# Wider gaps between the rows of three DRAM scratch buffers in an FFT convolution kernel

## The chip, the core and the metric

The kernel runs on one core of a Trainium2 chip. The metric is the time on the device in microseconds (us), as the median of several executions. One further execution was recorded by the hardware profiler; all durations of single instructions and transfers come from that one.

The engines are named as the profile names them: PE is TensorE (matrix multiply; its weight loads are PEld), DVE is VectorE, ACT is ScalarE, POOL is GpSimd, and SP is SyncE, which here only starts DMA transfers. Transfers started by SP and ACT run in hardware queues (q1 and q10 in the profile), those started by POOL in a software queue (q0). All of them are carried out by the core's 16 DMA engines.

## What is computed

The input x is (4, 512, 512, 16) in float32: four images of 512 by 512 points with 16 channels. There are two layers, each x + layer(group norm(x)). The first is a convolution with a 512 by 512 filter per pair of channels that is given as a quotient of two polynomials, done by Fourier transform; the second is a 3 by 3 cosine-similarity convolution. Cut to what matters:

```
a = pad(denominator, ones), b = pad(numerators, zeros)          # 9 x 9 taps each
h = irfft2(rfft2(b, (512, 512)) / rfft2(a, (512, 512)))         # impulse response, 512 x 512
H = h0 + rfft2(h, (1024, 1024))                                 # per (in channel, out channel)
X = rfft2(gn(x), (1024, 1024));  Y = einsum("...hwi,ijhw->...hwj", X, H)
x = x + irfft2(Y, (1024, 1024))[:512, :512]                     # layer 0
x = x + cosine_conv3x3(gn(x))                                   # layer 1: arccos, tanh gates, bias
```

## The kernel before, in words

`body` (L1390) runs four phases one after the other. They hand data on through DRAM buffers, and the change concerns the layout of three of these.

**The buffers.** `g_d` (the filter), `x_d` (the transformed image) and `y_d` (the product) are each four DRAM tensors with 128 rows (L1391 to L1393). A row of `g_d` holds 1 MiB: 128 *places* of 8192 bytes (16 output channels j times 128 numbers). A row of `x_d` or `y_d` holds 256 KiB. The tensors are declared `PITCH` = 1024 elements wider than their content (L56), so that one row starts 4096 bytes further on than the content of the row before would end. The helper `dram(t, row, offset, *dims)` (L197) builds the access patterns: with a row given it addresses inside that row; with `None` it puts the 128 rows first, a row pitch apart, one for each SBUF partition.

**filter_phase** (L231) computes the filter pair by pair. Per output channel j, `placed` (L404) copies results into a staging tile `st` and, after eight pairs, stores it with four transfers (two halves a, two q) at L416: 128 partitions, 16 places for each, 512 bytes at each place. `odd(j)` (L422) then loads such pieces back as `ev_in` (`load`, L432, transfers at L436: 128 partitions, 4 places, 512 bytes), multiplies them with `todd` (L450), copies the result to `ot` (L455) and stores it with the same pattern into the other two tensors (L456). So all of `g_d` is written in pieces of 512 bytes, and half of it is also read in such pieces. The order of PE, DVE, ACT and POOL is fixed by hand with the class `InOrder`; SP issues its transfers in the order that the program's scheduler gives.

**forward_phase** (L604) transforms the images, and stores at L687 to `x_d` with 128 rows, 16 places 2048 bytes apart, 512 bytes each.

**conv_phase** (L697) goes over 513 filter rows (row 0 is done in two planes). In step n, SP starts four kinds of loads. `load_x(n + 3)` (L749) reads one whole row of `x_d`, 256 KiB. `load_g(n + 2)` (L737, the planes at L740) reads one whole row of `g_d`, 1 MiB, one place of 8192 bytes to each partition. `load_xe(n + 1)` (L816) reads 3 MiB from the small DRAM buffers `xf_d`, as two transfers of 1.5 MiB. Their content was computed one step earlier: `x_part` and `x_late` (L785) multiply the image row, and POOL stores it in two parts (L792, `xf_d<-xe` and `xf_d<-xl`). `xf_d` has rows of 4096 bytes at a pitch of 4608 bytes (`XP`, L58); it is not part of the change. PE does in four quarters of a step: `mix` (L846, the channel product, which reads `xe` and `gh`), `g_part` (L830, the filter's transform along the row, which reads the tile `g`), `over_q` (L867); once per step also `x_part` (L778) and `over_g` (L904), whose result POOL stores as one whole row of `y_d` (L915). The tiles `g` and `x` have two buffers, `xe` has three.

**last_phase** (L964) transforms back: for each of 16 n, eight tiles `yt` of 1 MiB are loaded at L1134 from `y_d` (128 rows, 8192 bytes from each), multiplied (L1143), and stored by ACT's queue (L1155). From n = 9 on the group norm of the second layer is prepared beside it (`prepare`, L1041), and then the 3 by 3 convolution runs.

The two address computations that the change rewrites in the filter phase are these:

```python
out=dram(g_d[h], None, a * G_ROW // 2 + ((32 * q + 16 * kp) * C + j) * 8 * C,
         [C * 8 * C, 16], [1, 8 * C]),
...
return [((first[c] + 4 * (tb % 8)) * C + j) * 8 * C for c in range(2)]
step = [C * 8 * C, 4], [1, 8 * C]
```

Of the kernel before, what the change touches and what calls it, by code (L numbers as in the profile page):

```python
# [46 lines left out]
P = 128  # L47
N = 512
B = 4
C = 16  # L50
S = 64
F = 128
G_ROW = 2 * S * C * 8 * C
X_ROW = 2 * S * B * 8 * C
Y_ROW = 2 * B * S * C * 8
PITCH = 1024  # L56
XF = F * 2 * B
XP = XF + 128  # L58
GN_EPS = 1e-5
# [137 lines left out]
def dram(t, row, offset, *dims):  # L197

    pitch = t.shape[1]
    lead = [[pitch, t.shape[0]]] if row is None else []  # L200
    return bass.AP(tensor=t.tensor, offset=t.offset + (row or 0) * pitch + offset,
                   ap=lead + [list(d) for d in dims])
# [28 lines left out]
def filter_phase(tc, cst, h0, num, den, g_d, beside):  # L231
    nc = tc.nc
    with ExitStack() as ctx:
# [170 lines left out]
        def placed(pair, st, pg):  # L404

            kp, i, h, j = (pair[0][k] for k in ("kp", "i", "h", "j"))
            for u in range(2):
                for a in range(2):
                    nc.scalar.copy(  # L409
                        st[a].rearrange("p (q k u x) i -> p u k q x i", q=2, k=2, u=2)[:, u, :, :, :, i : i + 2],  # L410
                        pg[u][:, :, :, 2 * a : 2 * a + 2].rearrange("p n k q x -> p k q x n"),
                    )
            if i == C - 2:
                for a in range(2):
                    for q in range(2):
                        nc.sync.dma_start(  # L416
                            out=dram(g_d[h], None, a * G_ROW // 2 + ((32 * q + 16 * kp) * C + j) * 8 * C,
                                     [C * 8 * C, 16], [1, 8 * C]),
                            in_=st[a].rearrange("p (q r e) i -> p q r (e i)", q=2, e=8)[:, q],
                        )  # L420

        def odd(j):  # L422

            def place(tb):
                first = ((0, 96), (64, 32))[tb // 8]
                return [((first[c] + 4 * (tb % 8)) * C + j) * 8 * C for c in range(2)]

            step = [C * 8 * C, 4], [1, 8 * C]  # L430

            def load(tb):  # L432
                ev = evp.tile([P, 2, 2, 32 * C], F32, name="ev_in")
                for h in range(2):
                    for c in range(2):
                        nc.sync.dma_start(  # L436
                            out=ev[:, h, c].rearrange("p (s e) -> p s e", s=4),
                            in_=dram(g_d[h], None, place(tb)[c], *step),
                        )
                return ev  # L440

            ev = load(0)
            for tb in range(16):
                after = load(tb + 1) if tb < 15 else None
                for hh in range(2):
                    ot = odp.tile([P, 2, 32 * C], F32, name=f"ot{hh}")
                    for c in range(2):
                        pt = ps_t.tile([P, 32 * C], F32, name="pt", tag="t")
                        for kc in range(2):
                            nc.tensor.matmul(  # L450
                                pt, todd[:, c, kc, hh * P : hh * P + P], ev[:, kc, c],
                                start=(kc == 0), stop=(kc == 1),
                            )
                        yield
                        nc.scalar.copy(ot[:, c], pt)  # L455
                        nc.sync.dma_start(  # L456
                            out=dram(g_d[2 + hh], None, place(tb)[c], *step),
                            in_=ot[:, c].rearrange("p (s e) -> p s e", s=4),
                        )
                ev = after  # L460

        def odds():

            for j in range(C):
                while done[0] < 64 * (j + 1) + 8:
                    yield
                yield from odd(j)
# [11 lines left out]
        for p in range(n_pairs + 2):  # L479
# [3 lines left out]
            if last:  # L483
                if last[0]["i"] == 0:
                    st = [stp.tile([P, N // 2, C], F32, name=f"st{a}", tag="st") for a in range(2)]
                with order:
                    for w in last:
                        edge(w)
                    placed(last, st, taps(last))
                done[0] += 2  # L490
                for w in last:
                    w.clear()
# [9 lines left out]
            with order:  # L502
# [6 lines left out]
                j, kp, r = p // 32, p // 16 % 2, p % 16  # L509
# [187 lines left out]
def conv_phase(tc, cst, g_d, x_d, y_d):  # L697
    nc = tc.nc
    with ExitStack() as ctx:
# [32 lines left out]
        def load_g(n):  # L732
            rc, r, plane = rows[n]
            g = io.tile([P, C, 8 * C], F32, name="g")
            t, w = g.rearrange("p j x -> p (j x)"), C * 8 * C
            if plane is None:
                nc.sync.dma_start(out=t, in_=dram(g_d[rc], r, 0, [w, P], [1, w]))  # L737
            else:
                for to, at in ((0, (0, 96)[plane]), (64, (64, 32)[plane])):
                    nc.sync.dma_start(out=t[to : to + 32], in_=dram(g_d[rc], r, at * w, [w, 32], [1, w]))  # L740
                    nc.gpsimd.memset(t[to + 32 : to + 64], 0.0)
            state["g", n] = g

# [179 lines left out]
        def step(n):  # L923
# [7 lines left out]
            if row(2):  # L931
                load_g(n + 2)
# [457 lines left out]
def body(tc, ins, cst, out):  # L1390
    g_d = [tc.dram_tile([P, G_ROW + PITCH], F32, name=f"g_d{r}") for r in range(4)]  # L1391
    x_d = [tc.dram_tile([P, X_ROW + PITCH], F32, name=f"x_d{r}") for r in range(4)]
    y_d = [tc.dram_tile([P, Y_ROW + PITCH], F32, name=f"y_d{r}") for r in range(4)]  # L1393
    yw_d = [tc.dram_tile([C, N, N], F32, name=f"yw_d{b}") for b in range(B)]
    t_d = [[tc.dram_tile([N, P, C], F32, name=f"t_d{b}_{w}") for w in range(4)] for b in range(B)]
    with tc.tile_pool(name="s_mv", bufs=2 * B) as mp:
        mvs = []
        with tc.tile_pool(name="s_in", bufs=1) as xp:
            beside = image_stats(tc, xp, mp, ins["x"], mvs)
            filter_phase(tc, cst, ins["L0_conv_h0"], ins["L0_conv_numerators"][0],  # L1400
                         ins["L0_conv_denumerator"], g_d, beside)
            for _ in beside:
                pass
        forward_phase(tc, cst, ins["x"], mvs, x_d)
    conv_phase(tc, cst, g_d, x_d, y_d)
    last_phase(tc, cst, ins["x"], y_d, yw_d, t_d, ins["L1_conv_kernel"], ins["L1_conv_bias"],
               ins["L1_conv_radius"], out)
# [30 lines left out]
```

## Time and profile before

| | us |
|---|---|
| median of 3 runs | 16582.36 |
| lowest and highest of them | 16561.65, 16588.23 |
| the profiled execution, its own time | 16601.06 |
| its span, first to last instruction | 16599.1 |
| filter phase, about 0 to 3950 | 3950 |
| forward phase, about 3950 to 4750 | 800 |
| conv phase, about 4750 to 13750 | 9000 |
| back transform, about 13750 to 14900 | 1150 |
| 3 by 3 convolution, about 14900 to the end | 1700 |

The profiled execution took 1.96 us more than its span, and 18.7 us more than the median. The granted TensorE clock was 0.973 of full speed over the span. The program has 2703070 packets in the hardware queue that SP feeds; a packet is one contiguous piece that one DMA engine moves.

How to read it: "busy" of an engine is the time in which it executes instructions, as a share of the span or of the window asked for. The DMA share is the mean busy share of the 16 DMA engines. A group line gives what is written and read (`out<-in`), count, busy time, mean duration in ns, idle time of the engine before it, and what ended most of that idle time. A wait line says who waited for whom, the total in us, how many times, and the longest.

### The profile page before, as it was taken

To read this page: it belongs to the slowest core of one execution; us is meant where nothing else is said; L and a number is where in the kernel's file an instruction comes from. 1 tells how busy PE (TensorE), PEld (TensorE's weight loads), DVE (VectorE), ACT (ScalarE), POOL (GpSimd) and SP (SyncE) were. 2 spreads that over 40 slices of the span, in tenths; PEclk is the share of its full clock that TensorE was granted. 3 is DMA by queue.
4 is the path that set the end of the run, shared out by engine and by line. 5 is a ranking of instruction groups with operands and counts; after the bars stand their busy time and mean duration, and the time that the engine had idled before them with its cause. 6 is when DMAs were issued, how large, how long until landed. Compare 5 with 4: busy or idle time off the path is not lost. (4 is left out here: it accounts for less than half of the span.)

```text
span 16599.1 us, 545650 instructions
## 1 busy us (share of the span) xinstructions
PE 15057.2 (91%) x232588; PEld 11240.5 (68%) x232588; DVE 10596.9 (64%) x22299; ACT 9042.9 (54%) x18799; POOL 10362.7 (62%) x10669
## 2 busy tenths in 40 slices
PE   7999999998988899889899989898888888988888
PEld 5555555554557777777777777777777777767777
DVE  8999999993545555555555555555555552357877
ACT  5666666663345555555555555555555551027888
POOL 7777777772346666666666666666666660237766
PEclk7999999999999999999999999999999999989999
DMA  4888888878878888888888888888888886885531
GB/s 134 233 235 236 232 238 235 240 226 257 253 262 327 321 328 326 326 326 323 326 328 320 328 325 329 325 323 327 319 325 328 321 324 236 309 289 167 165 108 69
DMA packets 2914698, 4543.40 MB, mean 274 GB/s; under 512 B 126114, under 2 KB 2094460, under 8 KB 2801422
## 3 DMA queue, kind: packets, MB, share of 16 engines
q1 hardware_dynamic: 2703070, 3836.37, 67.4%
q0 software_dynamic: 172336, 605.00, 9.4%
q10 hardware_dynamic: 36864, 67.13, 1.2%
q8 instruction: 1833, 30.03, 0.7%
q14 instruction: 595, 4.87, 0.1%
HBM read 3030.71 MB, written 1477.31 MB: 272 GB/s over the span
## 5 line engine op out<-in xcount | busy, mean ns | idle before, releaser
L830 PE MATMUL pg<-c_dg,g 64*128 64x128 f32 x32832 | 2851.6, 290 | 372.2 <-ACT gh L730 220.5
L846 PE MATMUL pm<-xe,gh 128*32 128x64 f32 x131328 | 2370.2, 222 | 486.0 <-issue 234.5
L830 PEld LDWEIGHTS pg<-c_dg,g 64*128 64x128 f32 x32832 | 2293.3, 189 | 716.2 <-ACT gh L730 278.1
L846 PEld LDWEIGHTS pm<-xe,gh 128*32 128x32 f32 x131328 | 1998.2, 110 | 1072.6 <-issue 838.6
L875 DVE TENSOR_TENSOR z<-zq,pz 128x256 f32<-128x256 f32 x2052 | 859.4, 419 | 2695.4 <-ACT zq L874 2641.7
L728 DVE COPY gh<-pg 128x512 f32<-128x512 f32 x2046 | 1408.3, 688 | 1148.2 <-PE pg L830 1144.1
L450 PE MATMUL pt<-ev_in,c_todd 128*128 128x512 f32 x4096 | 1927.3, 609 | 109.0 <-ACT u L338 83.4
L799 POOL TENSOR_TENSOR xu<-xe,c_late 128x256 f32<-128x256 f32 x2052 | 1392.2, 702 | 845.6 <-ACT xe L730 826.7
L507 DVE RECIPROCAL dn<-dn 128x256 f32<-128x256 f32 x1024 | 1716.9, 1716 | 0.0
L730 ACT COPY yf<-pm 128x512 f32<-128x512 f32 x2046 | 1211.9, 592 | 901.5 <-PE pm L846 887.9
L382 POOL TENSOR_TENSOR sp<-m,dn 128x512 f32<-128x512 f32 x1024 | 1301.1, 1272 | 615.0 <-DVE dn L507 528.8
L810 ACT COPY xe<-xl 64x1024 f32<-64x1024 f32 x513 | 539.1, 1051 | 1892.1 <-POOL xl L801 1892.1
L450 PEld LDWEIGHTS pt<-ev_in,c_todd 128*128 128x128 f32 x4096 | 728.6, 190 | 1021.8 <-issue 704.3
L730 ACT COPY gh<-pg 128x512 f32<-128x512 f32 x2058 | 1201.2, 584 | 356.7 <-PE pg L830 355.1
L867 PE MATMUL pz<-c_ident,yf 128*128 128x128 f32 x8208 | 1365.6, 289 | 27.1 <-issue 14.1
L398 PEld LDWEIGHTS pg<-c_dinv,sp 64*128 64x128 f32 x16384 | 1004.5, 196 | 464.6 <-ACT sp L387 210.8
L409 ACT COPY st<-pg 128x256 f32<-128x256 f32 x2048 | 617.2, 391 | 1281.2 <-PE pg L398 1281.2
L801 POOL TENSOR_TENSOR xl<-xl,xu 128x1024 f32<-128x1024 f32 x513 | 1210.0, 2359 | 40.2
L398 PE MATMUL pg<-c_dinv,sp 64*128 64x128 f32 x16384 | 1106.7, 287 | 70.4 <-ACT sp L387 47.4
L1281 PE MATMUL pc<-l_band,xn 128*128 128x160 f32 (+2 forms) x6144 | 1078.0, 334 | 50.7 <-DVE e_o L1336 50.4
L883 POOL TENSOR_TENSOR zd<-z 128x512 f32<-128x512 f32 x513 | 653.6, 1274 | 742.4 <-DVE z L875 742.3
L915 POOL DMA_DIRECT2D y_d<-yo x511 | 296.5, 580 | 1305.0 <-ACT yo L730 1279.1
(211 smaller groups left out, 30874.7 us busy)
## 6 DMA issues: line engine op xcount, KB each, us to landing
xe<-xf_d SPq DMA_DIRECT2D x1026, 1536.0 KB
g<-g_d SPq DMA_DIRECT2D x511, 1024.0 KB
g_d<-st SPq DMA_DIRECT2D x256, 1024.0 KB
ev_in<-g_d SPq DMA_DIRECT2D x1024, 256.0 KB
g_d<-ot SPq DMA_DIRECT2D x1024, 256.0 KB
xf_d<-xe POOLq DMA_DIRECT2D x513, 448.0 KB, 8.2
xf_d<-xl POOLq DMA_DIRECT2D x513, 448.0 KB, 5.5
x_d<-xo SPq DMA_DIRECT2D x128, 1024.0 KB
```

Source lines behind the costliest of these rows:

```text
L382: nc.gpsimd.tensor_mul(w["sp"], w["m"], bc(w["dn"], 2, [P, 2, 2, P]))
L398: nc.tensor.matmul(pg[u][:, n, k].rearrange("p a x -> p (a x)"), w["sp"][q, k, c, :], dinv[q, 2 * kp + k, c, :], start=(c == 0), stop=(c = ...
L450: nc.tensor.matmul(pt, todd[:, c, kc, hh * P : hh * P + P], ev[:, kc, c], start=(kc == 0), stop=(kc == 1),)
L507: nc.vector.reciprocal(w["dn"], w["dn"])
L728: nc.vector.tensor_copy(dst, src)
L730: nc.scalar.copy(dst, src)
L799: nc.gpsimd.tensor_mul(u[:, :, h, c], xe[:, :, h, 1 - c], bc(late[:, 1 + c], 2, [P, F, 2]))
L801: nc.gpsimd.tensor_add(xl.rearrange("p f h c k -> p (f h c k)"), xl.rearrange("p f h c k -> p (f h c k)"), u.rearrange("p f h c k -> p (f ...
L830: nc.tensor.matmul(pg[c][:, j % 4], g[half, j], dg[half], start=True, stop=True)
L846: nc.tensor.matmul(pm[32 * q : 32 * q + 32, g % 8], gh[:, f].rearrange("p c j -> p (c j)"), xe[:, :, f].rearrange("p t h c k -> p t (h c k ...
L867: nc.tensor.transpose(pz[:, t % 4].rearrange("p v q x -> p (v q x)"), y[:, at].rearrange("p g x -> p (g x)"), ident)
L1281: nc.tensor.matmul(pc[:, lo:hi, :].rearrange("p w j -> p (w j)"), xns[q][:, h * P + dh : h * P + dh + P], bands[dh][:, o : o + hi - lo, :] ...
```

## The change

The places of a `g_d` row lie 8704 bytes apart instead of 8192: a new constant `GP` is 128 elements (512 bytes) larger than a place's content, and every address into `g_d` uses it. A row's content with its gaps thus takes 1114112 bytes instead of 1048576. `PITCH` grows from 1024 to 1152 elements, that is from 4096 to 4608 bytes, for `g_d`, `x_d` and `y_d`. From row to row `g_d` goes from 1052672 to 1118720 bytes, and `x_d` and `y_d` go from 266240 to 266752 bytes. All of it is address arithmetic: no instruction, tile or computed number is added or removed.

```diff
-G_ROW = 2 * S * C * 8 * C
+GP = C * 8 * C + 128
+G_ROW = P * GP
...
-PITCH = 1024
+PITCH = 1152
...
-                            out=dram(g_d[h], None, a * G_ROW // 2 + ((32 * q + 16 * kp) * C + j) * 8 * C,
-                                     [C * 8 * C, 16], [1, 8 * C]),
+                            out=dram(g_d[h], None, a * G_ROW // 2 + (32 * q + 16 * kp) * GP + j * 8 * C,
+                                     [GP, 16], [1, 8 * C]),
...
-                return [((first[c] + 4 * (tb % 8)) * C + j) * 8 * C for c in range(2)]
-
-            step = [C * 8 * C, 4], [1, 8 * C]
+                return [(first[c] + 4 * (tb % 8)) * GP + j * 8 * C for c in range(2)]
+
+            step = [GP, 4], [1, 8 * C]
...
-                nc.sync.dma_start(out=t, in_=dram(g_d[rc], r, 0, [w, P], [1, w]))
+                nc.sync.dma_start(out=t, in_=dram(g_d[rc], r, 0, [GP, P], [1, w]))
...
-                    nc.sync.dma_start(out=t[to : to + 32], in_=dram(g_d[rc], r, at * w, [w, 32], [1, w]))
+                    nc.sync.dma_start(out=t[to : to + 32], in_=dram(g_d[rc], r, at * GP, [GP, 32], [1, w]))
```

## The prediction, made before the changed kernel was run

> **What bounds the kernel now.** I read the page first, then busy time by stage (us, busy time and instructions of PE, PEld, DVE, ACT and POOL, PE clock, DMA share, GB/s).
>
> ```profile
> span 16599.1 us, 545650 instructions
> PE 15057.2 (91%) x232588; PEld 11240.5 (68%) x232588; DVE 10596.9 (64%) x22299; ACT 9042.9 (54%) x18799; POOL 10362.7 (62%) x10669
> ```
>
> ```profile
> 300.00:3900.00 3600.00, 3485.57 (x28864) 2017.13 (x28863) 3203.24 (x4292) 2298.28 (x6399) 2638.78 (x3032) 1.00 0.82 236
> 3950.00:4750.00 800.00, 779.92 (x2496) 398.99 (x2496) 429.50 (x560) 273.39 (x499) 311.06 (x66) 1.00 0.78 238
> 4750.00:13750.00 9000.00, 8069.67 (x184617) 6466.92 (x184621) 4911.84 (x13312) 4771.16 (x8714) 5779.08 (x5641) 0.98 0.87 324
> 13950.00:14900.00 950.00, 840.47 (x3880) 727.41 (x3880) 391.78 (x1086) 129.99 (x298) 216.36 (x133) 0.95 0.83 290
> ```
>
> PE is busy 97% of the filter and forward stages, 90% of the conv stage (third row). DMA is busy 82, 78, 87 and 83%: high enough that each stage must be asked whether transfers end a wait. In the filter stage they hardly do; these are its longest waits for DMA:
>
> ```profile
> PEld pt L450 <- DMA ev_in<-g_d: 52.2, 163, 1.5
> ACT ot L455 <- DMA g_d<-ot: 30.7, 17, 8.6
> PEld pt L450 <- DMA g_d<-ot: 18.2, 61, 0.3
> ```
>
> In the conv stage the chain lies in one step, seen in the timeline (start us, us):
>
> ```profile
> 8000.87 0.37 SPq L816 DMA_DIRECT2D xe<-xf_d  x1
> 8001.03 1.10 PE L846 MATMUL pm<-xe,gh 128*32 128x64 f32 x64 [2.75 <-DMA xe<-xf_d]
> 8001.33 0.46 SPq L737 DMA_DIRECT2D g<-g_d  x1
> 8001.85 0.42 SPq L816 DMA_DIRECT2D xe<-xf_d  x1
> ...
> 8014.88 0.58 POOL L792 DMA_DIRECT2D xf_d<-xl  x1 [0.29 <-POOL xl L801]
> ...
> 8018.42 0.37 SPq L816 DMA_DIRECT2D xe<-xf_d  x1
> ```
>
> PE waited 2.75 us for `xe`; SP then starts half of the next `xe`, the 1 MiB of `g`, and the other half. So `g` lies in the queue ahead of data that the next row needs. The stage's SP and PE waits and its queues (packets, MB, share of 16 engines):
>
> ```profile
> SPq L816 <- DMA xf_d<-xl: 6606.7, 512, 15.1
> ```
>
> ```profile
> PE pm L846 <- DMA xe<-xf_d: 83.9, 74, 3.0
> ```
>
> ```profile
> q1 hardware_dynamic: 561699, 2287.33, 68.3%
> q0 software_dynamic: 172096, 604.21, 17.4%
> ```
>
> From the trace's packet records, sorted by queue and size: an `xe` load takes 14.9 us (median) from issue to its last packet, out of a row of 9000 / 513 = 17.5 us, and between 1 and 14 us after issue the 16 engines are full. In 189 of 513 rows the first matmul of L846 starts less than 1 us after the last `xe` packet; PE's idle time just before these sums to 157 us. In the other rows the transfer has slack (median of all: 1.5 us) and engines set the row. So the conv stage is bound partly by DMA, and a shorter `g` transfer can count there.
>
> **What the Trainium skill says.** "DMA: Bandwidth & Descriptors", section "Latency and other measured facts": copies with a 4 MiB row pitch ran at 103 GB/s, with 4 KiB more at 214, with 192 bytes more at 97. Every buffer here already has 4 KiB beyond a power of two per row, and the trace agrees that the large effect is gone: 1531509 packets of 512 bytes (300 to 3900 us) have a mean of 28.4 ns and a median of 27. Same page, "How a descriptor splits into AXI transactions": a piece is cut into 256-byte transactions, and only a start off a 256-byte boundary costs more. 8704, 4608 and the new row pitches are multiples of 256. The trace agrees for 4608: `xe`, whose DRAM rows have this pitch, has a median of 159 ns for 4096 bytes (25.8 GB/s an engine). Same page, "Issuing engines are not separate DMA queues": SP's and POOL's transfers share the 16 engines; the two shares above add to 86% of the same engines.
>
> **The change part by part.** Program order and waits on all five engines are the same in both kernels. What moves is DRAM addresses.
>
> *Filter stores and loads (L416, L456, L436).* Same 512-byte pieces. Mean 28.4 against median 27 ns: what better addresses could win is 1.4 x 1531509 / 16 = 134 us of all engines, but under a PE that is 97% busy; the cover is the idle 18% of the DMA engines. I take 0; at best the 101 us of waits shown, of which little is PE's own. If pieces got slower, the cover goes at 28.4 / 0.82 = 34.6 ns.
>
> *Forward stores (L687).* Pitch 266752 instead of 266240, same pieces; PE 780 of 800 us busy. 0, covered by the 22% that DMA is idle.
>
> *Load of a `g` row (L737).* Packets stay 8192 bytes: other loads with gaps between rows (`yt`, 260 KiB apart) come in 8192-byte packets too. 65536 such packets have a mean of 346 ns and a median of 309: the excess is 37 x 128 / 16 = 296 ns a row. It grows within a load from 314 (first 16 packets) to 379 (seventh 16), also while no other queue moves data, whereas `xe` packets settle at 160 to 165. That hints at addresses, which 512-byte gaps would spread. Against it: in the filter stage the DMA engines also work at equal residues (4 partitions apart are 4 MiB + 16 KiB) and are at their floor. So from both sides: nothing, or all 0.3 us, with another 0.13 us since the second half of `xe` starts at 187 ns a packet behind the tail of `g` and settles at 163; and below nothing, see rivals. I take half of the excess, 0.15 us a row. In the rows bound by DMA the gain is the smaller of 0.15 us and PE's idle time there, summed over the 189 rows: 27 us. Next late after that are ACT's and DVE's evictions (L730, L874), which rows with slack already wait for. As rows with slack are no shorter (17.5 us) than bound ones (17.4), part comes back; I keep 25.
>
> *`x_d` rows and `y_d` rows, whole.* Their packets are contiguous before and after; only starts move by 512 bytes a row. `x` packets have 85 against 84 ns: 0.
>
> *Loads of `yt` (L1134).* 8192-byte packets at 328 against 309 ns from 13950 to 14900: 16384 x 19 / 16 000 = 19 us of full engines, beside ACT, DVE and PE waits. I take 5; from 0 to 12.
>
> *Bases.* `g_d` grows by 33.8 MB, so `xf_d` and later buffers move. No row prices this; I take 0, inside the range.
>
> Sum: 25 + 5 = 30 us less. The profiled execution took 16601.1 (span 16599.1 plus 2.0), so it would take 16571; the median of the runs is 18.7 lower: 16582 - 30 = 16552.
>
> **The rivals.** About 0.2% (33 us) is what a measurement of this kernel can tell from no change.
>
> *All of the excess goes.* 0.43 us a row, over the bound rows 73 us, plus 12 for `yt`: 16582 - 85 = 16497. For: `xe` at a pitch of 4608 is near its floor when alone, `g` at 8192 is not. Against: medians are at the floor already, and damping. It can reach 130 less if shifting the row loop also frees later waits.
>
> *Slower: `g` loads get slower.* The mechanism is at L737: `g` stands between the halves of `xe` in a full queue, so 10% more a packet (35 ns) adds 0.28 us to each `xe` load; rows lose what exceeds their slack, by the records 48 us: 16630. It decides from 25 ns on (0.2 us a row, 32 us). For: a row is no longer one contiguous 1 MiB, and no run shows this pitch. Against: `xe` and `yt` with gaps are not slow.
>
> *The change does nothing.* Bytes, packets and order are the same, and a tail of slow packets appears in all 8192-byte loads, so its cause may be the full engines: 16582. This lies in my forecast's own band.
>
> **How the numbers follow.** Forecast (between 0 and 33 us less, or up to 33 more with nothing changed): 0.42, of which 0.12 is the third rival. All of the excess goes: 0.38. Slower: 0.20. So faster by over 0.2% 0.38, within it 0.42, slower 0.20. The range goes from 112 less (16470; 0.06 of the first rival lies below) to 58 more (16640; 0.07 of the second lies above). The likeliest case's own range is 16549 to 16615, its lower part likelier.
>
> **What would show it.** Right: conv stage down by some 25 us; q1's share there from 68.3 to about 67.5% (half of 37 ns x 65536 packets is 0.85% of 16 engines for 9000 us); PE's wait for `xe` from 84 to about 60 us; filter and forward stages unchanged within 5 us. First rival: `g` packets near 318 ns, q1 near 66.5%. Second: q1 over 69%, the wait over 100 us. The forecast is wrong if the filter stage moves, for then 512-byte pieces do depend on these gaps, or if `xe` packets change, for then the moved bases count.

## The result, and the profile after

The changed kernel takes 16531.24 us (median of 7 runs, 16521.11 to 16581.71), the kernel before 16582.36 us beside it. The ratio is 0.9974, with a 95% interval of 0.9962 to 0.9986: a small gain, some 40 us. The prediction said 16552, with "within 0.2%" as the likeliest outcome (0.42) and faster than that as the next (0.38); the measured 0.26% lies in the second, though its interval reaches into the first. The number was near; the reasons given for it were not, so it came near by luck.

The same windows of the profile after (columns as before: us, busy time and instructions of PE, PEld, DVE, ACT, POOL, then PE clock, DMA share, GB/s), below its span:

```profile
span 16529.3 us, 545650 instructions
```

```profile
300.00:3900.00 3600.00, 3490.41 (x28880) 2019.54 (x28878) 3203.97 (x4294) 2301.67 (x6405) 2640.64 (x3032) 1.00 0.80 237
3950.00:4750.00 800.00, 775.44 (x2482) 397.04 (x2481) 419.96 (x554) 273.41 (x499) 309.79 (x67) 0.99 0.79 239
4750.00:13750.00 9000.00, 8060.52 (x184678) 6458.88 (x184676) 4920.08 (x13346) 4773.14 (x8720) 5780.93 (x5650) 0.99 0.87 324
13950.00:14900.00 950.00, 853.51 (x4097) 741.32 (x4096) 432.09 (x1165) 179.16 (x378) 267.00 (x190) 0.96 0.85 302
```

In the filter stage the DMA share fell from 82 to 80% at the same rate. In the conv stage nothing moved: 87% and 324 GB/s as before. The waits and queues that the prediction had named for it (who waited for whom, us in total, times, longest; then packets, MB, share) say the same:

```profile
SPq L817 <- DMA xf_d<-xl: 6582.2, 512, 15.1
```

```profile
PE pm L847 <- DMA xe<-xf_d: 83.1, 71, 3.2
```

```profile
q1 hardware_dynamic: 561494, 2288.16, 68.3%
q0 software_dynamic: 172336, 605.00, 17.5%
```

The wait for `xe` is 83.1 us (83.9 before) and q1's share 68.3% (68.3). By the packet records a `g` packet of 8192 bytes takes 345.0 ns (345.7). The step that carried most of the predicted gain, faster `g` packets, did not happen at all.

Where the stages begin and end can be read from the first and last start of three groups (line, engine, tiles, count: duration ns min/median/max, first to last start in us, form): the last product of the filter stage, the first and last channel product of the conv stage, the last store of the back transform. Before:

```profile
L450 PE MATMUL pt<-ev_in,c_todd x4096: 592/592/1222, 298.1 to 3907.2; 128*128 128x512 f32 x196
...
L846 PE MATMUL pm<-xe,gh x131328: 216/219/316, 4786.8 to 13750.1; 128*32 128x64 f32 x200
...
L1155 ACTq DMA_DIRECT2D yw_d<-yo x256: 524/525/812, 13828.6 to 14830.4; - x128
```

After:

```profile
L451 PE MATMUL pt<-ev_in,c_todd x4096: 592/592/1193, 298.6 to 3898.1; 128*128 128x512 f32 x196
...
L847 PE MATMUL pm<-xe,gh x131328: 216/219/316, 4775.1 to 13717.0; 128*32 128x64 f32 x200
...
L1156 ACTq DMA_DIRECT2D yw_d<-yo x256: 524/525/626, 13797.1 to 14768.1; - x128
```

So the filter stage ends 9.1 us earlier (3907.2 to 3898.1), the conv stage is 21.4 us shorter (8963.3 to 8941.9), and the time from its end to the last store of the back transform is 29.3 us shorter (1080.3 to 1051.0). Which of the three belongs to the change is a question for the experiments.

### The profile page after: what moved, and what is told of

It reads as the page before. It is cut to its first block, busy times and chain, and to the rows that moved or that the text cites. A ratio compares the mean times of both kernels' runs of the same rounds, so it can differ in the third digit from the quotient of the medians.

```text
span 16529.3 us, 545650 instructions
## 1 busy us (share of the span) xinstructions
PE 15017.5 (91%) x232588; PEld 11213.2 (68%) x232588; DVE 10598.9 (64%) x22299; ACT 9042.0 (55%) x18799; POOL 10365.1 (63%) x10669
## 5 line engine op out<-in xcount | busy, mean ns | idle before, releaser
L868 PE MATMUL pz<-c_ident,yf 128*128 128x128 f32 x8208 | 1362.8, 289 | 27.4 <-issue 12.6
## 6 DMA issues: line engine op xcount, KB each, us to landing
g<-g_d SPq DMA_DIRECT2D x511, 1024.0 KB
g_d<-st SPq DMA_DIRECT2D x256, 1024.0 KB
x_d<-xo SPq DMA_DIRECT2D x128, 1024.0 KB
```

The lines of the kernel that those rows point to most:

```text
L868: nc.tensor.transpose(pz[:, t % 4].rearrange("p v q x -> p (v q x)"), y[:, at].rearrange("p g x -> p (g x)"), ident)
```

## The experiments

Two theories stood against each other after the result. One: gaps in the layout make transfers faster, in `g_d` or in `y_d`. The other: the larger buffers only move what is allocated behind them, and transfers with one of those buffers are faster at its new place. A third had to be excluded first: that the difference lies in the granted clock (0.973 and 0.975 in the two profiled executions).

Stage times in this table are differences of the starts named above; packet times are means of the trace's packet records (filter: 512-byte packets from 300 to 3900 us; from 300 to 5500 us in the kernel without gaps; `p_y`: 512-byte packets from its first load to the last store of the back transform). Each ratio is to runs of the kernel before made beside it; each stage time comes from one profiled execution.

| kernel | ratio to before (95%) | filter us | conv us | back us | filter packet ns | p_y packet ns |
|---|---|---|---|---|---|---|
| before | 1 | 3907.2 | 8963.3 | 1080.3 | 28.4 | 36.7 |
| after | 0.9974 (0.9962 to 0.9986) | 3898.1 | 8941.9 | 1051.0 | 27.5 | 31.3 |
| after, again | 0.9976 (0.9963 to 0.9988) | 3895.5 | 8941.0 | 1046.7 | 27.5 | 31.0 |
| places only | 0.9993 (0.9985 to 1.0002) | 3896.7 | 8935.2 | 1078.3 | 27.5 | 36.1 |
| pitch only | 0.9972 (0.9964 to 0.9981) | 3896.1 | 8968.3 | 1051.9 | 27.4 | 31.5 |
| starts only | 0.9977 (0.9969 to 0.9984) | 3904.9 | 8940.1 | 1048.9 | 28.3 | 31.0 |
| yw_d and t_d moved 0.75 MiB | 0.9997 (0.9989 to 1.0005) | 3906.6 | 8981.5 | 1083.3 | 28.3 | 36.6 |
| t_d moved | 0.9998 (0.9990 to 1.0006) | 3905.3 | 8953.9 | 1077.4 | 28.3 | 35.3 |
| yw_d moved 0.3125 MiB | 0.9972 (0.9961 to 0.9984) | 3909.8 | 8964.8 | 1053.4 | 28.5 | 31.7 |
| yw_d planes apart | 0.9967 (0.9955 to 0.9980) | 3908.9 | 8964.9 | 1031.4 | 28.3 | 28.0 |
| half of g_d's rows | 0.9994 (0.9986 to 1.0002) | 3900.7 | 8979.2 | 1092.3 | 28.0 | 38.1 |
| after, g issued late | 0.9967 (0.9956 to 0.9978) | 3896.9 | 8968.4 | 1054.1 | 27.5 | 30.9 |
| after, planes apart | 0.9954 (0.9941 to 0.9966) | 3899.5 | 8981.7 | 1024.0 | 27.5 | 28.0 |
| no gaps | 1.0966 (1.0951 to 1.0981) | 5507.6 | 8959.3 | 1088.5 | 45.6 | 37.5 |

### First set: the parts of the change

After, again: the changed kernel, unaltered.

> The changed kernel once more, beside the kernel before on one chip. If the change itself makes the difference, the ratio is again near 0.997 (some 50 us), with the same marks in the profile: 512-byte packets of the filter stage at 27.5 instead of 28.4 ns, p_y's 512-byte packets in the back transform at 31 instead of 37 ns. If the difference was a matter of the granted clock (0.973 before, 0.975 after in the profiled executions), the ratio is 1.000 within 0.1% and the clocks of the two kernels are equal.

The ratio came out at 0.9976, with the two marks. The granted clocks overlap (0.972 to 0.975 in its runs, 0.971 to 0.975 in those of before). In the filter stage the clock is full in both kernels (1.00 in the windows), and PE's busy time from 300 us to the stage's end is 3492 us before and 3489 after: of 9 us, at most 3 can come from the clock. So the clock alone is not the cause there; for the back transform the second set decides.

Places only (against the changed kernel, like the next two):

```diff
-PITCH = 1152
+PITCH = 1024
```

> Only the places of g_d are 8704 bytes apart; the rows' gap stays 4096 bytes. If the places make the gain: filter packets of 512 bytes at 27.5 ns, the stage 5 to 10 us shorter, and all of the ratio (0.997) if the moved bases count as well, since yw_d moves here too (by 33.6 MB). If the pitch of y_d makes the gain of the back transform, p_y's packets stay at 37 ns and some 30 us of the gain are missing (ratio 0.999).

Pitch only:

```diff
-GP = C * 8 * C + 128
+GP = C * 8 * C
```

> Only the rows of g_d, x_d and y_d get the gap of 4608 bytes; the places stay 8192 apart and the bases move by less than 1 MB. If the pitch of y_d makes the gain in the back transform: p_y at 31 ns, back transform 30 us shorter, ratio 0.998. If the bases or the places do it: p_y at 37 ns, ratio 1.000.

Starts only (layouts of before in buffers of the changed size; x_d and y_d likewise):

```diff
+    def moved(name, content, more):
+        t = tc.dram_tile([P, content + PITCH + more], F32, name=name)
+        return Rows(t.tensor, t.offset, (P, content + PITCH))
-    g_d = [tc.dram_tile([P, G_ROW + PITCH], F32, name=f"g_d{r}") for r in range(4)]
+    g_d = [moved(f"g_d{r}", G_ROW, P * 128 + 128) for r in range(4)]
```

> Every address pattern as in the kernel before, but g_d, x_d and y_d are allocated as large as in the changed one, so that yw_d, t_d and xf_d lie where they lie there. If the moved base of yw_d makes the gain in the back transform: p_y at 31 ns and 30 us less (ratio 0.998), filter packets at 28.4 ns. If the layouts do it: p_y at 37 ns, ratio 1.000.

The hardware queue in the filter stage, 300 to 3900 us (packets, MB, share of 16 engines), in the kernel before, with the places alone, and with moved starts alone:

```profile
q1 hardware_dynamic: 1579466, 844.74, 81.0%
```

```profile
q1 hardware_dynamic: 1583877, 847.22, 79.2%
```

```profile
q1 hardware_dynamic: 1581272, 845.64, 81.0%
```

With the places, slightly more packets take less of the engines' time; with moved starts the share stays.

Read by columns, the table separates two effects. The filter stage gets 8 to 12 us shorter in every kernel with a wider gap in `g_d`, be it between the places or between the rows, and not with moved starts alone. The back transform gets 28 to 34 us shorter in the changed kernel, with "pitch only" and with "starts only", whose layout is that of before, and not with "places only". So it does not need the layout of `y_d`; it needs a moved start. The addresses in the built programs show which: no buffer there crosses a multiple of 256 MiB, so the four `g_d` and `xf_d` stay where they were in all these kernels. What moves is `x_d` by up to 8 MiB, `y_d` by 64 to 256 KiB, and `yw_d` from 1186.5 to 1186.8125 MiB with some of `t_d` behind it; in "places only" `y_d` and `yw_d` stay. (The expectations above still took it that everything behind `g_d` moves by 33 MB. That was wrong.)

### Second set: which buffer, and does a shorter g load pay

Both moves were made by allocating the buffer ahead larger, without using the rest:

```diff
-    y_d = [tc.dram_tile([P, Y_ROW + PITCH], F32, name=f"y_d{r}") for r in range(4)]
+    y_d = [tc.dram_tile([P, Y_ROW + PITCH], F32, name=f"y_d{r}") for r in range(3)]
+    t = tc.dram_tile([P, Y_ROW + PITCH + 1536], F32, name="y_d3")
+    y_d.append(Rows(t.tensor, t.offset, (P, Y_ROW + PITCH)))
```

> The kernel before, with 0.75 MiB left free after y_d, so that yw_d, t_d and xf_d lie 0.75 MiB further on; every layout is that of before. If the gain of the back transform comes from where yw_d or t_d starts within a MiB (806.75 MiB after y_d's end with the change, 774.0 before): p_y's 512-byte packets at 31 ns, back transform 1050 us instead of 1080, ratio 0.998. If it takes the move by 33 MB or of y_d itself: 37 ns, 1080 us, ratio 1.000.

> The kernel before, with 0.75 MiB left free between yw_d and t_d: only t_d and xf_d move. If t_d's place against yw_d or the input counts: p_y at 31 ns and 30 us less. If yw_d's own start counts: 37 ns, 1080 us, ratio 1.000.

Neither did anything: 1.000, with `p_y` at 36.6 and 35.3 ns. The first of these texts worked from addresses that are not those of the built programs: the run had `yw_d` at 1187.25 MiB, where the changed kernel has 1186.8125. So these two runs show only that these places do not help. (`xf_d` moves in neither.)

```diff
-    yw_d = [tc.dram_tile([C, N, N], F32, name=f"yw_d{b}") for b in range(B)]
+    yw_d = [tc.dram_tile([C, N * N + 1152], F32, name=f"yw_d{b}") for b in range(B)]
+    yw_d = [t[:, : N * N].rearrange("c (h w) -> c h w", h=N) for t in yw_d]
```

> The kernel before, with yw_d's 16 planes 4608 bytes further apart (1 MiB + 4608 bytes instead of 1 MiB). p_y's load reads 512 bytes from each of eight planes in turn. If the slow p_y packets come from the power-of-two step between planes: 27 to 29 ns instead of 37, back transform 1040 us or less, ratio 0.997. If the start of the buffer is all that counts, the packets stay near 37, or at 31 by the accident of the new start.

This hit: `p_y` at 28.0 ns, back transform at 1031.4 us, ratio 0.9967. The load of `p_y` (L1052) takes 512 bytes from each of eight planes that lie exactly 1 MiB apart; with the planes 4608 bytes further apart, its packets are nearly as fast as those of the filter stage. This is not a moved start in another guise: for the image whose `yw_d` comes first, and starts at 1186.5 MiB in both kernels, `p_y`'s packets alone went from 36.5 to 28.3 ns. Nor is it the stores into the same planes: their packets of 2048 bytes took 87.7 ns before and 90.8 after. The stretch from the first `p_y` load to the last store, in the kernel before, the changed one and this one (columns as above):

```profile
14107.00:14830.00 723.00, 624.61 (x2748) 536.04 (x2746) 316.27 (x921) 65.62 (x174) 185.54 (x82) 0.95 0.90 315
```

```profile
14076.00:14768.00 692.00, 615.91 (x2746) 531.28 (x2744) 318.27 (x922) 65.65 (x174) 186.20 (x82) 0.96 0.93 329
```

```profile
14113.00:14786.00 673.00, 613.30 (x2746) 529.57 (x2746) 324.89 (x922) 65.64 (x174) 186.21 (x82) 0.97 0.95 339
```

The work is the same (2748, 2746 and 2746 matmuls), DMA is at 90% or more, and the rate goes from 315 to 329 to 339 GB/s. Here the transfers set most of the pace: from before to the changed kernel, 68608 packets of 512 bytes at 36.7 - 31.3 = 5.4 ns less are 23 us of all 16 engines, and the stretch got 31 us shorter. PE's own busy time fell by 8.7 us in it, at a clock of 0.96 instead of 0.95; the rest is idle time that went.

The fourth kernel of this set is the changed one with `g`'s load moved behind both halves of `xe`:

```diff
             if row(3):
                 load_x(n + 3)
-            if row(2):
-                load_g(n + 2)
             if row(1):
                 load_xe(n + 1)
...
                 if row(2) and k == 0:
+                    load_g(n + 2)
                     for m in range(B):
```

> The changed kernel, with the load of a g row issued after both halves of xe instead of between them. It tests the term by which the prediction turned a shorter g transfer into time: xe should land some 2.8 us earlier in each row and PE's wait for xe in the conv stage (83 us in the changed kernel) should all but vanish. By the model of the prediction the conv stage then loses about the idle time before the first matmul of the bound rows, 100 to 150 us (ratio 0.989 to 0.991 to before). If engines set the row anyway, the wait goes and the conv stage stays within 20 us of 8942.

By the packet records `xe` now lands 11.8 us after its issue instead of 14.9, and no row starts within 1 us of its last packet. PE's wait for `xe` is gone from its longest waits; instead there is one for `g`:

```profile
PE pm L847 <- issue: 284.5, 312, 3.5
PE pg L831 <- ACT gh L731: 201.8, 232, 3.8
...
PE pg L831 <- DMA g<-g_d: 66.1, 87, 2.0
```

The conv stage took 8968.4 us, in the scatter of all others (8935 to 8982), and the ratio (0.9967) cannot be told from the changed kernel's 0.9974. So three us less per `xe` load, twenty times what the prediction hoped for, gave no shorter stage. But the window of 4750 to 13750 us (columns as above) shows that this is not the same as no effect:

```profile
4750.00:13750.00 9000.00, 8111.21 (x184656) 6473.53 (x184655) 4920.84 (x13330) 4778.83 (x8716) 5782.23 (x5641) 0.98 0.87 324
```

For as many matmuls as in the changed kernel (184656 and 184678) PE was busy 51 us longer. From the first to the last channel product it stood idle for 882 us, less than in any of the other thirteen traces (905 to 948), and was busy for 8087 us, more than in any (8015 to 8047): its clock records show half the full clock for 349 us of the stage, against 215 to 273. So some of the shorter wait did become less idle time, and slower matmuls took it back. Whether the moved load brought the lower clock or chance did is not shown.

And `g`'s packets went to 327.7 ns with the same addresses: about half of their excess over the median of 309 came from what ran ahead of them or beside them.

### Third set: the start of yw_d alone, the filter stage, both together, and no gaps

Moved by 0.3125 MiB, with `t_d` put back on a multiple of 0.25 MiB (as above, 640 instead of 1536, and a rest of 0.4375 MiB behind `yw_d`):

> The kernel before, with 0.3125 MiB left free after y_d and 0.4375 MiB after yw_d. yw_d then starts where it starts in the changed kernel (the built programs have it at 1186.8125 MiB there, at 1186.5 before; the run that moved it by 0.75 MiB had it at 1187.25), while g_d, x_d, y_d and their layouts are those of before and t_d stays at a multiple of 0.25 MiB. If yw_d's own start makes the gain in the back transform: p_y's 512-byte packets at 31 ns, back transform near 1050 us, ratio 0.998. If the moved starts of y_d or t_d make it: 37 ns, 1080 us, ratio 1.000.

The start of `yw_d` was the cause: 1053.4 us, 31.7 ns, ratio 0.9972. (`t_d` lies where it lay in the first run of the second set, which gained nothing.) The table as a whole agrees: with that start and planes 1 MiB apart the back transform takes 1047 to 1054 us in six kernels, with any other start 1077 to 1092 in six.

```diff
-    g_d = [tc.dram_tile([P, G_ROW + PITCH], F32, name=f"g_d{r}") for r in range(4)]
+    g_d = [tc.dram_tile([P, G_ROW + (1024, 1152)[r // 2]], F32, name=f"g_d{r}") for r in range(4)]
```

> The kernel before, with the gap of 4608 bytes for the rows of g_d 2 and 3 alone, which the stores of ot write; the tensors that st's stores write and ev_in's loads read keep 4096. y_d and yw_d stay where they are. If ot's stores make the filter stage's gain: 512-byte packets near 27.5 ns and the stage 8 to 11 us shorter. If the others do: 28.4 ns, no gain. If all share it: about half of each. The ratio is too small a measure for it (0.9995); the stage in the profile decides.

About half: packets at 28.0 ns (28.4 and 27.5 at the ends), stage 6.5 us shorter, where kernels with the gaps of before scatter by 5 us (3904.9 to 3909.8); ratio not separable from 1. By the packets the effect is shared by the stores of `ot` and the other transfers of 512 bytes.

The changed kernel with `yw_d`'s planes apart, by the edit shown above:

> The changed kernel with yw_d's planes 4608 bytes further apart: the two causes found, together. If they add: filter stage 3897 us, back transform 1031 us, p_y at 28 ns, ratio 0.996 (some 60 us less than before). If the changed start of yw_d had already taken part of what the planes give, the ratio is that all the same, since the planes' run alone had 1031 us; a ratio above 0.997 would say that they don't add.

They add: filter stage 3899.5, back transform 1024.0, ratio 0.9954 (0.9941 to 0.9966), the best of all kernels measured.

Last, `PITCH = 0` in the kernel before. The row of the Trainium skill that the text below names stands in "DMA: Bandwidth & Descriptors", section "Latency and other measured facts"; its 40 ns for pieces of 512 bytes are an estimate from it:

> The kernel before without any gap beyond a row's content: g_d's rows at 1 MiB, x_d's and y_d's at 256 KiB. It shows how much the gap of 4096 bytes already gave, and so whether the step to 4608 could be large. By the Trainium skill's row on pitches at large powers of two, packets of 512 bytes in the filter stage at 40 ns or more, which fills the DMA engines and makes the stage longer by several hundred us; yt's packets in the back transform slower too. If the gaps hardly count at these pitches: within 1% of before.

The filter stage's last product shows what it did (columns as above):

```profile
L450 PE MATMUL pt<-ev_in,c_todd x4096: 592/592/1222, 296.8 to 5507.6; 128*128 128x512 f32 x196
```

The stage took 5507.6 us instead of 3907.2; no other stage changed by more than the scatter. The median product takes 592 ns as before. Most of the stage from 300 us on (columns as above):

```profile
300.00:5500.00 5200.00, 3846.91 (x28861) 2134.95 (x28859) 3208.99 (x4289) 2312.66 (x6396) 2648.85 (x3030) 0.86 0.88 164
```

Its longest waits for DMA there:

```profile
PE pt L450 <- DMA ev_in<-g_d: 937.9, 227, 30.8
ACT ot L455 <- DMA g_d<-ot: 822.9, 86, 17.7
PEld pt L450 <- DMA ev_in<-g_d: 586.8, 267, 7.2
```

In the kernel before, the same three rows stood at 15.4 (the row `PE pt <- DMA ev_in`, not among those shown), 30.7 and 52.2 us. The packets of 512 bytes take 45.6 ns, and the DMA share of that stretch is 0.88 at 164 GB/s. From 300 us to the end of the stage PE's idle time grew from 115 to 1353 us, and its busy time, for the same matmuls, from 3492 to 3855 us at a granted clock of 0.86 instead of 1.00. So the gap of 4096 bytes that was there already is worth 1600 us, some 360 of them as longer busy time at the lower clock, and the step to 4608 another 8 to 12. Without gaps the buffers also start elsewhere (the third and fourth of `g_d` at 384 and 512 MiB instead of 512 and 768); no run separates that from the pitch.

## Why the prediction was near, point by point

**Filter stage: predicted 0, measured 8 to 12 us less.** The packets' excess of 1.4 ns was there to win and 0.9 was won. The bound given from above (some share of the 101 us of waits) held. The same three waits in the changed kernel (before, in this order: 52.2, 18.2, 30.7):

```profile
PEld pt L451 <- DMA ev_in<-g_d: 57.2, 196, 1.1
PEld pt L451 <- DMA g_d<-ot: 18.2, 65, 0.3
ACT ot L456 <- DMA g_d<-ot: 15.9, 9, 5.5
```

ACT's wait for an `ot` buffer halved, by 14.8 us; PE's own for `ev_in` went from 15.4 to 9.8, while that of its weight loads rose by 5. How these add up to 9 us is not shown. DMA was 82% busy on average and yet late now and then; an average below 100% is not full cover. The price at which the cover would go, 34.6 ns a packet, has a counterpart in the kernel without gaps, at 45.6 ns and with 1600 us more; in between no run was made.

**Forward stage: predicted 0, measured 1 to 3 us less** in the two profiles of the changed kernel, which its scatter hides. Right.

**Load of a g row: predicted 27 us, 25 kept; measured nothing that shows.** This is the step that failed: "I take half of the excess, 0.15 us a row". The excess stayed: 345.7 ns a packet before, 345.0 and 354.7 in the two profiles of the changed kernel, 353.7 with the places alone. The signs named for it stayed too (q1's share 68.3%, the wait for `xe` 83 us). The hint was misread: that packets slow down within a load "while no other queue moves data" left out the neighbours in the same queue, and with `g` behind `xe` they were faster at equal addresses. The run with the places alone also bounds the gain: its ratio allows 25 us in all, of which the filter stage took 10. The conversion, 0.15 us a row into PE's idle time, was therefore never put to use. The run that took 3 us from each `xe` load leaves it open. PE's idle time before the first product of a row fell from 232 us in all (changed kernel) to 94. But PE then waited 66 us for `g`, and for ACT's evictions as long as before (202 us, 199 in the changed kernel). Over the stage it stood idle for 23 to 66 us less than in the other traces, and no shorter stage came of it. The prediction had a sign of this in hand, rows with slack being no shorter than bound ones, and cut 27 only to 25 for it. The 21 us by which the conv stage looks shorter after the change are scatter: kernels with the old places range from 8940 to 8982, those with the new ones from 8935 to 8982.

**x and y rows, whole: predicted 0.** `x` packets took 84.7 to 84.9 ns in every trace. Right.

**Loads of yt: predicted 5 us; measured nothing of that kind.** The packets of 8192 bytes in that stretch went from 329 to 338 ns, slower, while the rate of the stretch rose from 315 to 329 GB/s. That their neighbours crowded closer is likely, and not shown.

**Bases: "I take 0".** This is where most of the gain came from: 27 to 34 us, by a start of `yw_d` 0.3125 MiB further on. The prediction named the possibility, gave no price, and was wrong on what moves and how far (by 33 MB; `xf_d` does not move at all). It also said that "Every buffer here already has 4 KiB beyond a power of two per row". That holds for the three buffers of the change, not for `yw_d`: `p_y`'s loads take their pieces of 512 bytes at a step of exactly 1 MiB. The diff does not touch them, and they stand in a stretch with DMA at 90%.

So two terms of 25 and 5 us that did not come were made up for by two of about 10 and 30 that were put at zero. That the sum came near is luck. As an account of the mechanism the prediction was wrong, and its own test for that came true: it is wrong "if the filter stage moves".

**Row pitches.** The Trainium skill, "DMA: Bandwidth & Descriptors", section "Latency and other measured facts", has copies of tiles with 16 KiB per row at 207 GB/s with a pitch of 512 KiB, 164 with 2 MiB and 103 with 4 MiB; it has no figure for 1 MiB or for pieces of 512 bytes. The runs agree that such a pitch costs: at 1 MiB, 45.6 against 28.4 ns a packet in the filter stage (1.6 times), and 36.7 against 28.0 at the planes of `yw_d` (1.3 times). The row calls 4 KiB more full rate (214 GB/s); here another 512 bytes still took 0.9 ns off a packet. For the row pitch of 256 KiB no run shows a loss: without gaps in `x_d` and `y_d` the forward stage and the back transform stayed within 9 us.

What stays open: why `yw_d` does better at 1186.8125 MiB than at 1186.5 or 1187.25, while its planes are 1 MiB apart in all three. The two slow starts are multiples of 0.25 MiB, as is 896 MiB, where `yw_d` starts in the kernel without gaps (37.5 ns); a second start off these multiples was not tried. With the planes apart the question matters little (28.0 ns from either start).

## What to carry to other kernels

When buffers change size, look at where the ones behind them come to lie, and price transfers by their whole address pattern, including those the diff doesn't touch: here the ones with a step of 1 MiB between small pieces were where addresses counted. The first gap in such a pattern was worth far more than a second one, so ask which gap is still missing before widening one that is there. And before turning a shorter transfer into time, check that rows not bound by it are really shorter. When a wait goes and the time stays, read idle and busy time apart: the granted clock can take back what the wait gave.

## What the runs showed of the hardware that had not been expected

Pieces of 512 bytes at a step of 1 MiB between rows or planes took 45.6 ns (filter stage) and 36.7 ns (`p_y`), against 27.5 and 28.0 with gaps of a few KiB; 8192-byte rows 256 KiB apart showed no such loss (back transform before `p_y`'s loads: 323.7 ns a packet without gaps, 323.0 with). And moving a buffer by 0.3125 MiB with no change of layout was worth 5 ns a packet in that same pattern. In the filter stage without gaps, where PE idled for 1353 of 5208 us, its granted clock was 0.86 instead of 1.00: late transfers came with slower matmuls as well.
